# Two outlook layers: 32 by 32 turns on VectorE, regrouped channels and one matmul per group average

## The chip, the cores and the metric

The kernel runs on one core of one Trainium2 chip. A core has TensorE (matmuls, which write to PSUM), VectorE, ScalarE and GpSimd for the rest, and SyncE, which here only issues transfers; 16 DMA engines move data between the chip's HBM and SBUF. In profiles they are PE (and PEld for its weight loads), DVE, ACT, POOL and SP. The metric is device microseconds of one launch. Inputs and outputs are float32 in HBM.

## The reference, cut to what matters

The input x is 8 images of 56 by 56 positions with 384 channels. Two layers follow each other, and each adds its result to x. Both begin with a group norm over 32 groups of 12 channels, whose mean and variance run over all positions of an image.

```python
def gn(v):                                   # per image and group of 12 channels
    return (g - mean(g)) / sqrt(var(g) + 1e-5)

# layer 0: 12 heads of 32 channels, 3x3 window, fold
v = gn(x) @ Wv.T
a = softmax((gn(x) @ Wa.T).reshape(b, n, 12, 9, 9) * 32 ** -0.5)
out = einsum('bnhpq,bnqhd->bnphd', a, windows(v))
y = sum of out[p] shifted to place p of the window     # canvas.at[...].add
x = x + y @ Wo.T

# layer 1: 6 heads of 64 channels, 3x3 window
a = softmax((gn(x) @ W_attn + b_attn).reshape(b, n, 6, 9))
v = gn(x) @ W_v + b_v
x = x + einsum('bpKhd,bphK->bphd', windows(v), a) @ W_proj + b_proj
```

## The kernel before, in words

Images are taken in pairs: four pairs of 2 x 56 = 112 rows (R), each of 56 columns (W). Matmuls contract over channels, so x is needed with channels on the 128 partitions (three chunks, NCH), while HBM holds it with channels innermost. TensorE turns it: a load puts 112 rows of four columns (a block, XB) on 112 partitions, and `stats_chunk` (line 443) turns one chunk of it with four transposes against the identity into a PSUM tile, which ScalarE copies to SBUF; VectorE's `bn_stats` takes the sums for the norm from the copy. Per block there are three such chunks, per pair 14 blocks. Chunk i holds channels 128 i to 128 i + 127. The turned blocks are kept in HBM (`xTs`, `keep_block`) and are loaded again twice: for the norm (`load`, `normed`) and as the residual (`load_res`).

Since a group of 12 channels can cross a chunk's border, `norm_params` (line 275) averages over groups with seven small matmuls against three matrices `gmat`, once for the mean and once for the variance; it runs once for each pair and layer.

Layer 0 is one loop of 224 + 3 steps, a step for a column (line 918). `attend` does a tile of 128 tokens: three matmul sets for the logits, each followed by VectorE's maximum and subtraction, then ScalarE's exponential, then a set for v. Between the sets other work is put in, in an order written out by hand (`between`, line 938): after the first the turning of the next pair's block (`turned`: one chunk a step from the fourth column of a pair on), the previous column's normalisation (VectorE) and products (GpSimd), and a job; after the second the `fold` matmuls (pw) of an earlier column and the `bn_stats` of the turned chunk; after the third another job. The PSUM banks of the sets are three in turn. Softmax weights and values go to tables in HBM (`ztab0`, `vtab0`) and come back as patches: bands of weights z and values vp, by SyncE. `plan` (line 791) gives the jobs of seven columns their due steps: contractions pc of z and vp (ScalarE copies them to yT), then six projections po (two halves of the columns, three chunks each; `project_out`, line 833), whose result VectorE adds to the residual and writes to HBM (`x1s`). All po of layer 0 have one PSUM buffer, tag "o".

Layer 1 is a loop over 32 groups of seven columns, seven steps each (line 1218), with two jobs a step. `load` brings a group's x1t, `normed` scales it on ScalarE, `attend` does logits and v in one set, `fetch` (line 1143) loads z and vp for the group before the last one and puts its jobs in the queue: contractions two tiles at a time, with the turning of an earlier group's columns between them, then the projections. VectorE adds bias and residual in place in x1t. `turn` (line 1190) turns one column of it back with three transposes into PSUM, ScalarE copies to `ot`, and GpSimd issues the store of a half group, 112 rows of four or three columns with all 384 channels. Layer 1's first contractions are due three steps after their fetch.

Instructions that a helper records carry the helper's line: L118 are matmuls, L121 transposes on TensorE, L133 what VectorE, ScalarE, GpSimd and SyncE are given in a fixed order.

Of the kernel before, what the change touches and what calls it, by code (L numbers as in the profile page):

```python
# [15 lines left out]
def two_outlook_layers(  # L16
# [35 lines left out]
    P = 128  # L52
# [45 lines left out]

    xf = x.rearrange("b y x c -> (b y) x c")
# [12 lines left out]
    xTs = [dram.tile([P, NCH, W * R], F32, name=f"xT_{pair}") for pair in range(NPAIR)]  # L112
# [39 lines left out]
    near = [range(max(0, i - 1), min(NCH, i + 2)) for i in range(NCH)]  # L152
    gmat = [const.tile([P, len(near[i]), P], F32, name=f"gmat_{i}") for i in range(NCH)]
    with tc.tile_pool(name="ps_setup", bufs=2, space=PS) as ps_setup:
        gsel = yT_flat[:G, :C]
        gpsimd.memset(gsel, 1.0)
        gpsimd.affine_select(
            out=gsel, in_=gsel, compare_op=ALU.is_ge, fill=0.0,
            base=0, pattern=[[1, C]], channel_multiplier=-GC,
        )  # L160
        gpsimd.affine_select(
            out=gsel, in_=gsel, compare_op=ALU.is_ge, fill=0.0,
            base=GC - 1, pattern=[[-1, C]], channel_multiplier=GC,
        )
        for i in range(NCH):
            pg = ps_setup.tile([P, C], F32, tag="pg", name=f"pg_{i}")
            matmul(pg, gsel[:, i * P : (i + 1) * P], gsel, start=True, stop=True)
            lo, hi = near[i][0] * P, (near[i][-1] + 1) * P
            nc.vector.tensor_scalar_mul(gmat[i].rearrange("p j c -> p (j c)"), pg[:, lo:hi], 1.0 / GC)
# [93 lines left out]
    def weight(pool, src, n, name, queue=nc.sync):  # L263
        t = pool.tile([P, NCH, n], F32, name=name)
        queue.dma_start(t, src.rearrange("(i p) n -> p i n", p=P))
        return t

    def norm_params(st, name, params, key):

        mv = stat.tile([P, NCH, IMG, 2], F32, tag="mv", name=f"mv_{name}")  # L270

        def over_groups(src, what):
            pg = ps.tile([P, NCH, IMG], F32, tag="t", name=f"p{what}_{name}")
            for j in range(NCH):
                for i in near[j]:
                    matmul(
                        pg[:, j, :], gmat[i][:, j - near[i][0], :], src[:, i, :],
                        start=(i == near[j][0]), stop=(i == near[j][-1]),
                    )
            g = stat.tile([P, NCH, IMG], F32, tag=what, name=f"{what}_{name}")  # L280
            vector.tensor_copy(g, pg)
            return g

        for i in range(NCH):
            for b in range(IMG):
                vector.bn_aggr(mv[:, i, b, :], st[:, i, b, :, :])
        yield
        mean = over_groups(mv[:, :, :, 0], "gmean")

        part = stat.tile([P, NCH, IMG], F32, tag="part", name=f"part_{name}")  # L290
        vector.tensor_sub(part, mv[:, :, :, 0], mean)
        vector.tensor_mul(part, part, part)
        vector.tensor_add(part, part, mv[:, :, :, 1])
        yield
        var = over_groups(part, "gvar")
        std = stat.tile([P, NCH, IMG], F32, tag="std", name=f"std_{name}")
        scalar.activation(std, var, AF.Sqrt, bias=eps_t)
        scale = const.tile([P, NCH, IMG], F32, name=f"scale_{name}")
        vector.reciprocal(scale, std)
        bias = const.tile([P, NCH, IMG], F32, name=f"bias_{name}")  # L300
# [81 lines left out]
    zs = [patch.tile([P, NPY0, PY0 * ROW0], F32, name=f"z_{n}", bufs=1) for n in range(2)]  # L382
# [11 lines left out]
    scalar.dma_start(bo_t, bo1.rearrange("(i p) -> p i", p=P))  # L394
# [25 lines left out]
    def layer0(late, pools):  # L420
# [8 lines left out]
        def block_tile(tag, pair, blk):  # L429
            return io.tile([P, NCH, XB, R], F32, tag=tag, name=f"{tag}_{pair}_{blk}")  # L430

        def stats_load(pair, blk, queue, xr):
            queue.dma_start(xr, xf[pair * R : (pair + 1) * R, blk * XB : (blk + 1) * XB, :])
            xrs[pair, blk] = xr

        def xr_tile(pair, blk):
            return io.tile([P, XB, C], F32, tag="xr", name=f"xr_{pair}_{blk}")[:R]
# [5 lines left out]
        def stats_chunk(pair, blk, i):  # L443

            if blk == 0 and i == 0:
                stats[pair] = stat.tile([P, NCH, IMG, NBLK, 6], F32, tag="st0", name=f"st0_{pair}")
            if i == 0 and pair:
                xts[pair, blk] = block_tile("xt", pair, blk)
            xr, xt = xrs[pair, blk], xts[pair, blk]
            if pair == 0:  # L450
                pt = bank(P, 0, XB * R).rearrange("p (m r) -> p m r", m=XB)
            else:
                pt = ps.tile([P, XB, R], F32, tag="t", name=f"pt_{pair}_{blk}_{i}")
            for j in range(XB):
                transpose(pt[:, j, :], xr[:, j, i * P : (i + 1) * P], ident[:R, :R])
            scalar.copy(xt[:, i], pt)
            yield
            for b in range(IMG):
                vector.bn_stats(stats[pair][:, i, b, blk, :], xt[:, i, :, b * H : (b + 1) * H])
# [6 lines left out]
        def keep_block(pair, blk):  # L466
# [3 lines left out]
                    xTs[pair][:, :, blk * XB * R : (blk + 1) * XB * R],  # L470
                    xts.pop((pair, blk)).rearrange("p i m r -> p i (m r)"),
# [42 lines left out]
        for blk in range(NBLK):  # L514
# [5 lines left out]
            if blk == 1:  # L520
                wv_t = weight(fixed, wv0, C, "wv0_t", sync)
# [783 lines left out]
```

## Time and profile before

| | |
|---|---|
| median of 3 runs | 3312.41 us (3310.95 to 3320.32) |
| the profiled execution | 3315.84 us |
| its span, first to last instruction | 3314.0 us |
| TensorE, mean granted clock | 0.978 of full speed |
| TensorE transposes (L121) | 504 of xr for pairs 1 to 3, 168 of pair 0, 672 of results |
| DMA packets | 554,908, 850.99 MB, mean 257 GB/s; 162,174 of them under 512 B |

A profile lists for each engine what it was busy with and what it waited for. Rows of groups and of the timeline name the line, the engine, the operation, out<-in by the program's tile names, the shape and the count. In the timeline the first two numbers are start and length in us; rows that follow each other may overlap, because TensorE's instructions are pipelined, so what a set costs is the distance from its start to the next start. A bracket at the end is idle time before the row and what ended it. A float32 matmul leaves two records, a transpose one. The DMA share is the mean busy share of 16 engines; packets are contiguous runs.

### The profile page before, as it was taken

The page shows a single profiled execution, that of the slowest core. Times are in us where ns is not written, and L with a number is a line of the kernel's source. Part 1 is how long each engine was busy: PE and PEld are TensorE (multiplying, and loading weights), DVE is VectorE, ACT ScalarE, POOL GpSimd, SP SyncE. Part 2 cuts the span into 40 slices and gives each one's busy share as a digit, 9 for nine tenths or more (in the row PEclk, how much of TensorE's full clock was granted, in tenths as well). Part 3 has the DMA queues.
Part 4 walks back from the last instruction along what each step waited for, and adds up shares of the span by engine and source line. Part 5 has one row for each costly group of instructions (what it writes and reads, how often), then busy time and mean ns, then how long its engine had stood idle before and what let it go on. Part 6 is the DMA issues. An engine that isn't in the chain of part 4 may idle for free. (4 is left out here: it accounts for less than half of the span.)

```text
span 3314.0 us, 75237 instructions
## 1 busy us (share of the span) xinstructions
PE 3183.7 (96%) x28510; PEld 2186.6 (66%) x28510; DVE 1870.4 (56%) x4786; ACT 1366.3 (41%) x3749; POOL 1565.1 (47%) x2375
## 2 busy tenths in 40 slices
PE   7899999999999999999999999899999999999998
PEld 5567767776777667677666667556666666666665
DVE  5667776767777776777666677443333333333332
ACT  4444444444444444444343444234343443434432
POOL 2655555545555554455554555454343443434431
PEclk8899999999999999999999999899999999999999
DMA  9699988979897898899787888877778777787775
GB/s 294 201 308 295 303 274 270 292 258 304 300 315 235 279 308 266 290 294 300 229 257 259 288 253 294 285 240 212 220 215 233 212 216 226 220 222 214 223 215 155
DMA packets 554908, 850.99 MB, mean 257 GB/s; under 512 B 162174, under 2 KB 429954, under 8 KB 550450
## 3 DMA queue, kind: packets, MB, share of 16 engines
q1 hardware_dynamic: 448674, 672.76, 65.0%
q0 software_dynamic: 72016, 155.44, 14.7%
q10 hardware_dynamic: 33856, 17.98, 2.1%
q8 instruction: 225, 3.69, 0.5%
q14 instruction: 137, 1.12, 0.1%
HBM read 514.86 MB, written 322.17 MB: 253 GB/s over the span
## 5 line engine op out<-in xcount | busy, mean ns | idle before, releaser
L118 PE MATMUL bank<-wa_t,xn 128*128 128x288 f32 x3528 | 979.0, 415 | 3.5 <-ACT xn L133 2.1
L133 POOL TENSOR_TENSOR at<-at,den 128x972 f32<-128x972 f32 x196 | 440.5, 2247 | 859.3 <-DVE den L133 522.4
L118 PE MATMUL po<-yT,wo_t 128*128 128x448 f32 (+1 forms) x2304 | 821.0, 496 | 14.5 <-DVE x1t L133 12.0
L118 PEld LDWEIGHTS bank<-wa_t,xn 128*128 128x128 f32 x3528 | 652.9, 192 | 218.3 <-issue 22.2
L118 PEld LDWEIGHTS po<-yT,wo_t 128*128 128x128 f32 x2304 | 426.8, 191 | 296.0 <-issue 186.2
L133 ACT ACTIVATE at<-at 128x972 f32<-128x972 f32 (+1 forms) x228 | 215.8, 946 | 867.9 <-DVE at L133 860.5
L1075 POOL DMA_DIRECT2D at<-lgt x392 | 205.4, 527 | 616.3 <-DVE lgt L133 589.5
L118 PE MATMUL bank<-wc_t,xn 128*128 128x438 f32 x1176 | 477.8, 542 | 0.0
L133 DVE TENSOR_REDUCE mx<-bank 128x36 f32<-128x324 f32 x588 | 285.3, 485 | 340.6 <-PE bank L118 338.5
L118 PE MATMUL bank<-wv_t,xn 128*128 128x384 f32 x1176 | 417.3, 491 | 0.0
L118 PE MATMUL pc<-z,vp 121*32 121x49 f32 (+1 forms) x17664 | 374.7, 218 | 16.5 <-issue 10.3
L118 PEld LDWEIGHTS pc<-z,vp 121*32 121x32 f32 (+1 forms) x17664 | 337.8, 120 | 76.4 <-issue 51.0
L133 DVE TENSOR_TENSOR at<-bank,mx 128x324 f32<-128x324 f32 x588 | 291.4, 496 | 107.6 <-POOL pre L133 44.7
L118 PEld LDWEIGHTS bank<-wc_t,xn 128*128 128x128 f32 x1176 | 212.9, 190 | 169.4 <-issue 160.4
L118 PEld LDWEIGHTS bank<-wv_t,xn 128*128 128x128 f32 x1176 | 223.6, 192 | 134.8 <-issue 12.0
L133 DVE TENSOR_TENSOR lgt<-bank,ba_t 128x54 f32<-128x54 f32 x196 | 42.2, 215 | 455.8 <-PE bank L118 451.2
L133 POOL DMA_DIRECT2D vtab<-v x476 | 290.4, 614 | 14.4 <-issue 8.1
L133 ACT COPY yT<-pc 128x294 f32<-128x294 f32 (+2 forms) x512 | 195.7, 407 | 187.3 <-PE pc L118 186.4
L133 POOL TENSOR_TENSOR pre<-at,at 112x108 f32<-112x108 f32 (+1 forms) x440 | 224.4, 527 | 68.7 <-DMA at<-at 48.8
L133 DVE SCALAR_TENSOR_TENSOR x1t<-po,bo_t,x1t 128x448 f32<-128x448 f32 (+1 forms) x156 | 97.6, 626 | 249.5 <-PE po L118 249.5
L133 ACT COPY ot<-pt 112x384 f32<-112x384 f32 x128 | 61.2, 478 | 411.3 <-PE pt L121 411.0
L331 POOL DMA_DIRECT2D vtab<-v x392 | 211.4, 543 | 11.6 <-DMA vtab<-v 6.4
(118 smaller groups left out, 3279.0 us busy)
## 6 DMA issues: line engine op xcount, KB each, us to landing
z<-ztab SPq DMA_DIRECT2D x64, 2352.0 KB
vp<-vtab SPq DMA_DIRECT2D x64, 1536.0 KB
vp<-vtab SPq DMA_DIRECT2D x64, 945.0 KB
xres<-xT SPq DMA_DIRECT2D x32, 1176.0 KB
ztab<-wts SPq DMA_DIRECT2D x336, 110.2 KB
vtab<-v POOLq DMA_DIRECT2D x108, 336.0 KB, 6.2
xin<-xT SPq DMA_DIRECT2D x52, 672.0 KB
xr<-in_x SPq DMA_DIRECT2D x50, 672.0 KB
```

Of the source, the lines that this page charges most:

```text
L118: tc.keep_in_program_order(nc.tensor.matmul(*args, **kwargs))
L133: return lambda *args, **kwargs: tc.keep_in_program_order(op(*args, **kwargs))
L331: queue.dma_start(bass.AP(table.tensor, table.offset + first, [*([line * step, count] for step, count in rows_of or ((1, rows),)), *([[(R ...
L1075: nc.gpsimd.dma_start(at_of(g_of)[row : row + n, m_of].rearrange("r k h -> r (k h)"), lg[lo : lo + n])
```

## The change

Channels are regrouped and most turning is moved to another engine. Chunk i now holds the channels 3p + i, with p the partition, so that the 12 channels of a group lie on four partitions in each of the three chunks. `norm_params` then needs statistics per partition only (its `bn_aggr` runs over the three chunks), one matrix `gmat`, and one matmul for an average. Scale and bias depend on the partition alone, so `normed` covers all chunks in one instruction. Weights whose rows are channels are loaded accordingly; the columns of the two output weights are sorted by three copies each.

For pairs 1 to 3 the transposes of x are VectorE's, which works on 32 by 32 pieces within a quarter of the partitions. A load of a block becomes four, one for each quarter: a quarter takes 96 channels, and each of its 28 used lanes holds four rows, so HBM is read in runs of 96 channels. One VectorE instruction turns a chunk, in place of four transposes and a copy. Blocks in `xTs` are ordered by column, then chunk; the SBUF block has 128 places a row where 112 are stored. Results of layer 1 are turned in the same way after each projection, into an `ot` with four rows a lane, and stored by four SyncE transfers a half in place of one of GpSimd's. With `turn` gone, the contractions become one tile a job. The po tiles take the tags "o" and "t" in turn in both layers, and `attend` of layer 1 uses three banks.

```diff
+    Q = 32
+    NQ = P // Q
+    QC = NCH * Q
+    NR = 4
+    LANES = R // NR
+    def by_quadrant(ap, r0, col, n, b):
+        first = r0 * W * C + col * C + b * QC
+        return bass.AP(ap.tensor, ap.offset + first, [[W * C, R], [C, n], [1, QC]])
...
         def over_groups(src, what):
-            pg = ps.tile([P, NCH, IMG], F32, tag="t", name=f"p{what}_{name}")
-            for j in range(NCH):
-                for i in near[j]:
-                    matmul(
-                        pg[:, j, :], gmat[i][:, j - near[i][0], :], src[:, i, :],
-                        start=(i == near[j][0]), stop=(i == near[j][-1]),
-                    )
+            pg = ps.tile([P, IMG], F32, tag="t", name=f"p{what}_{name}")
+            matmul(pg, gmat, src, start=True, stop=True)
...
+            for b in range(NQ):
+                queue.dma_start(
+                    xr[b * Q : b * Q + LANES].rearrange("p s m c -> p (s m c)"),
+                    by_quadrant(x, pair * R, blk * XB, XB, b),
+                )
...
-                pt = ps.tile([P, XB, R], F32, tag="t", name=f"pt_{pair}_{blk}_{i}")
-            for j in range(XB):
-                transpose(pt[:, j, :], xr[:, j, i * P : (i + 1) * P], ident[:R, :R])
-            scalar.copy(xt[:, i], pt)
+                vector.transpose(
+                    xt[:, :, i, :].rearrange("p m (k s) -> p s m k", s=NR), xr[:, :, :, i::NCH]
+                )
...
-                    xTs[pair][:, :, blk * XB * R : (blk + 1) * XB * R],
-                    xts.pop((pair, blk)).rearrange("p i m r -> p i (m r)"),
+                    xTs[pair][:, blk * XB : (blk + 1) * XB].rearrange("p m i r -> p (m i) r"),
+                    xts.pop((pair, blk)).rearrange("p m i r -> p (m i) r")[:, :, :R],
...
-                po = ps.tile([P, 4 * R], F32, tag="o", name=f"po_{nm}_{half}_{j}")
+                po = ps.tile([P, 4 * R], F32, tag="ot"[(half + j) % 2], name=f"po_{nm}_{half}_{j}")
...
-                for t in range(0, (NPY1 + n_tile - 1) // n_tile, NC):
-                    jobs.add(due, lambda t=t, f=contract: [f(t + n) for n in range(NC)])
-                    jobs.add(due, turning.pop(0) if turning else lambda: None)
+                for t in range((NPY1 + n_tile - 1) // n_tile):
+                    jobs.add(due, lambda t=t, f=contract: f(t))
...
-            def turn(m):
-                pt = banks[-1][:R, :C] if m % 2 else ps.tile([R, C], F32, tag="t", name=f"pt1_{g}_{m}")
-                for i in range(NCH):
-                    transpose(pt[:, i * P : (i + 1) * P], x1t[:, i, m, :], ident)
-                scalar.copy(fetch.ot[:, m - lo, :], pt)
-                if m == hi - 1:
-                    nc.gpsimd.dma_start(
-                        of[pair * R : (pair + 1) * R, px * PX + lo : px * PX + hi, :],
-                        fetch.ot[:, : hi - lo],
-                    )
+                ot = fetch.ot[:, : NR * (hi - lo) * QC]
+                vector.transpose(
+                    ot.rearrange("p (s m c) -> p s m c", s=NR, c=QC)[:, :, :, j::NCH],
+                    bass.AP(x1t.tensor, x1t.offset + j * T + lo * R,
+                            [x1t.ap[0], [1, NR], [R, hi - lo], [NR, Q]]),
+                )
+                if j == NCH - 1:
+                    for b in range(NQ):
+                        later.append(
+                            lambda b=b: sync.dma_start(
+                                by_quadrant(out, pair * R, px * PX + lo, hi - lo, b),
+                                ot[b * Q : b * Q + LANES],
+                            )
+                        )
...
+    def sort_columns(t, by, i, engine):
+        engine(
+            t[:, i].rearrange("k (j p) -> k j p", j=NCH), by[:, i].rearrange("k (p j) -> k j p", j=NCH)
+        )
```

## The prediction

> **What bounds the kernel now.** I read the engine shares first, then the same split by stage, then the order of TensorE's work inside one stage, and last the DMA queues, since the change touches all of them. The stages are the first statistics pass (0 to 60 us), layer 0 on pairs 0 to 2 (to 1630), layer 0 on pair 3 (to 2150) and layer 1.
>
> ```profile
> PE 3183.7 (96%) x28510; PEld 2186.6 (66%) x28510; DVE 1870.4 (56%) x4786; ACT 1366.3 (41%) x3749; POOL 1565.1 (47%) x2375
> ```
>
> The same by stage, with the mean clock, the DMA engines' busy share and GB/s at the end of each row:
>
> ```profile
> core 0: us, PE busy (x) PEld busy (x) DVE busy (x) ACT busy (x) POOL busy (x), PEclk, DMA share, GB/s
> 0.00:60.00 60.00, 37.28 (x203) 31.56 (x204) 33.71 (x109) 24.21 (x49) 14.79 (x59) 0.77 0.98 303
> 60.00:1630.00 1570.00, 1509.86 (x14226) 1087.99 (x14225) 1123.68 (x2990) 688.42 (x1837) 818.77 (x1096) 0.98 0.86 281
> 1630.00:2150.00 520.00, 491.83 (x5038) 347.81 (x5036) 344.76 (x896) 204.88 (x562) 273.76 (x371) 0.96 0.82 268
> 2150.00:3314.00 1164.00, 1144.74 (x9046) 719.21 (x9046) 368.21 (x793) 448.77 (x1303) 457.81 (x850) 0.99 0.77 217
> ```
>
> TensorE is busy 96% in pairs 0 to 2 and 98% in layer 1. VectorE has room (72% and 32%). The 16 DMA engines have less than they seem to: 86% of pairs 0 to 2. A busy share isn't yet a bound, so the second question is what a transpose costs TensorE. Records overlap, so I take it from start to start in TensorE's timeline, not from durations: first three lines of layer 0, then layer 1.
>
> ```profile
> 1478.55 1.62 PE L118 MATMUL bank<-wa_t,xn 128*128 128x288 f32 x6
> 1480.01 0.55 PE L121 MATMUL pt<-ident,xr 112*128 112x112 f32 x4
> 1480.39 1.87 PE L118 MATMUL po<-yT,wo_t 128*128 128x336 f32 x6
> ...
> 2638.97 0.49 PE L121 MATMUL pt<-ident,x1t 128*112 128x128 f32 x3
> 2639.39 1.61 PE L118 MATMUL pc<-z,vp 90*64 90x56 f32 x48
> 2640.93 2.47 PE L118 MATMUL bank<-wc_t,xn 128*128 128x438 f32 x6
> 2643.24 0.49 PE L121 MATMUL bank<-ident,x1t 128*112 128x128 f32 x3
> 2643.66 1.26 PE L118 MATMUL pc<-z,vp 90*64 90x56 f32 x36
> ...
> 2653.71 0.54 PE L121 MATMUL pt<-ident,x1t 128*112 128x128 f32 x3
> 2654.76 2.52 PE L118 MATMUL po<-yT,wo_t 128*128 128x448 f32 x6 [0.51 <-ACT yT L133]
> ```
>
> The matmuls follow each other without a gap, and a set of transposes takes 0.38 us in layer 0 (1480.01 to 1480.39) and 0.42 in layer 1 (0.33 where a po follows). The last line matters too: where nothing but transposes stands between the last contraction and the projection that reads its yT, TensorE waits for ScalarE's copy. The queues:
>
> ```profile
> q1 hardware_dynamic: 448674, 672.76, 65.0%
> q0 software_dynamic: 72016, 155.44, 14.7%
> q10 hardware_dynamic: 33856, 17.98, 2.1%
> ```
>
> A share of 16 engines over 3314 us, divided by the packets, gives the engine time of one packet: q10 32.9 ns at 531 B, q1 76.8 ns at 1499 B, q0 108 ns at 2158 B. The first two give a line of 8.8 ns + 0.0453 ns/B, and it puts q0 at 106.6 ns. So small packets mostly cost their bytes.
>
> [...] No VectorE transpose is in this trace; the nearest rows are TENSOR_TENSOR of 432 elements at 606 ns and of 216 at 384, about 1.03 ns an element and 160 ns fixed[...]. [...]
>
> **The change part by part.**
>
> 1. *Transposes of x, layer 0, pairs 1 to 3* (done while pairs 0 to 2 are computed): 42 blocks x 3 sets leave TensorE: 126 x 0.385 = 48.5 us. A cross-check: pair 3, which has no sets, repeats its pattern after 512 us (1465.12 to 1977.00) where the earlier pairs need 523; 42 sets are worth 16 us, and that stretch holds two thirds of pair 3. The 168 transposes of pair 0, in the first 48 us, stay.
> 2. *Transposes of results, layer 1*: in one group of seven columns (32 groups) seven sets go, 4 x 0.42 less 0.08 that the entry of pc takes back, and 3 x 0.33, so 2.6 us. Against it stands the new order of the jobs. A contraction now does one tile, and they merge into five runs instead of four: +0.14 (a run costs 0.35 per twelve pairs of passes and 0.14 to start: 1.54 for four, 1.19 for three). And the last contraction stands right before projection (0, 0), with no transposes between: copy 0.31 and the hand-over, about 0.5 us. Net 1.9 x 32 = 60 us.
> 3. *Group averages*: 7 matmuls become 1, for mean and for variance, 8 times. At full clock 14 records take 1.48 us (1011.26 to 1012.74), at half clock some 3. Keeping about 0.3 each and the waits for VectorE's bn_aggr, whose input is the same in fewer instructions, leaves about 22 us.
> 4. *Two buffers for po in layer 0* (tags o and t): TensorE's waits for VectorE's x1t, 12.0 us in 16 places, mostly go: -9. What is late next there is the ztab store of the last columns, unchanged.
> 5. *The end*: ScalarE's copies and the four last sets go; three 0.6 us VectorE turns and four SP issues come: -4. The setup of gmat goes too (first transpose at 7.64), but the first pass is bound by loads (DMA 98%): 0.
> 6. *VectorE gains* 126 turns of 512 elements, 96 of 512 and 96 of 384. [...] An estimate throughout. I take 0.7 and 0.57: 88 us in pairs 0 to 2 (1124 + 88 = 1212 of about 1500, 81%) and 122 in layer 1 (42%). Hidden behind TensorE: in projecting steps of about 11 us VectorE idles 2 to 3.5 us. Behind each turn on VectorE stand normalise, then GpSimd's product and the pw matmul a step later: +0.7 us on the 14 places that already wait 34 us for pre. I allow +6.
> 7. *ScalarE* loses 126 copies (66.0 us), 224 copies (107 us) and two thirds of the norm instructions. It is no bound: 0. *GpSimd* loses 64 store issues (34.6 us): 0.
> 8. *DMA.* Loads of x become 4 issues of 448 packets of 384 B for 112 of 6144: per block 1792 x 26.2 / 16 = 2.9 us against 2.0 by the line[...]. Stores to xT become 1536 packets of 448 B, 2.8 against 2.2. Stores of out become 3136 packets of 384 B a group, 5.1 against 3.5[...]. With fewer, longer runs for xin and xres, 187,000 packets more in all. Pairs 0 to 2: 42 x 1.6 = 67 us; share x span goes from 1350 to 1417 of 1503 (1570 less 48.5 and some 18 of parts 3 and 4) = 94%[...]. Layer 1: 896 + 52 = 948 of 1100 = 86%. In 2 us slices full engines read 1.04, so this fits. The cover is lead time: in layer 1 the z bands are issued at 2693.48 and first read at 2708.72, 15 us for 1979 KB that need about 8; x has three steps (27 us). If that cover is gone, each us of lateness is one of TensorE. I allow +6.
> 9. *SP* gets 126 more load issues and 256 stores at about 0.5 us. Out stores wait for the third turn of a half. Behind them stand the next x1t load, needed five steps later, and the next z, six steps later: 0. They no longer compete from GpSimd's queue while z lands.
>
> 10. *Sorting wo's columns*: three copies of 384 elements on VectorE (layer 0) and three on GpSimd (layer 1), below 1 us each, well before the first projection reads them. The GpSimd copies wait for the load of wo1; GpSimd waits for that load today as well (18.2 us before the clearing of wz), and the logits stored behind it are read ten columns later: 0, and a few us at the turn between the layers if not.
>
> Sum: -48.5 - 60 - 22 - 9 - 4 + 12 = -131.5 from a span of 3314.0, so 3182. The profiled run is 3315.84, 1.84 over its span and 3.4 above the median of 3312.41; so the median should be about 3181. Since the two allowances are estimates from above, I say 3178.
>
> **The rivals.** *Likeliest, 0.66:* as summed, TensorE still the bound, 3140 to 3210.
>
> *DMA fills up in pairs 0 to 2, 0.14.* [...] Against: today slices of 0.92 and 0.93 stand beside a TensorE of 98 to 99.7%. Engine work there is 1350 - 184 (today's x and xT transfers, 42 x 4.4) + 8.7 us per ns of a new packet. Against 1503 x 1.04 it binds from 45 ns on; at 50 ns pairs 0 to 2 take 1540 and the kernel about 3215 to 3230. Range to 3290.
>
> *VectorE's order delays TensorE, 0.10.* At 2 us a turn VectorE is at 92%, and three banks no longer cover every step: 3195 to 3260. It is the bound outright from (1503 - 1124)/126 = 3.0 us.
>
> *Slower, 0.08:* packets of 384 B into and out of HBM cost far more than the line says, so that DMA bounds both layers. Work is 1166 + 8.7p in pairs 0 to 2 and 896 - 112 + 6.3p in layer 1; at a capacity of 1.04 both stages together take today's 2734 us when 1950 + 15p = 2843, p = 59.5 ns, and a little above that it decides. Against: q10's packets, most of them 504 B stores, cost 32.9.
>
> *No change, 0.02:* a loss that happens to meet the gain. That the transposes stay is excluded by the code.
>
> **How the numbers follow.** Within 0.3% (3302 to 3322) is what a measurement can't tell from no change. Faster 0.66 + 0.14 + 0.10 = 0.90, same 0.02, slower 0.08. The range 3140 to 3245 holds the first case, over half of the second and most of the third, some 0.8.
>
> **What would show it.** TensorE's only L121 records left are 168 in the first 50 us; pgmean and pgvar have 16 records each; VectorE transposes read 0.6 to 0.8 us; packets about 742,000; the layer 0 pattern of pairs 0 to 2 repeats after some 505 us instead of 523; a group of layer 1 is 1.9 us shorter and its first po waits about 0.5 us for ACT yT in nearly every group. The prediction is wrong if TensorE waits for VectorE's at or for z and vp, if the DMA share of pairs 0 to 2 reads 1.0 or more throughout, or if the turns take over 1.2 us.

## The result, and the profile after

The changed kernel takes 3285.99 us (median; 3282.16 to 3287.08) against 3316.36 for the kernel before on the same chip (3310.95 to 3324.34): a ratio of 0.990, 95% interval 0.988 to 0.993. It is faster by some 30 us, where 3178 had been predicted and a range of 3140 to 3245. The direction was right; three quarters of the gain are missing, and the time lies outside the range. Of the rivals only "DMA fills up" reaches so far (its range went to 3290), and its working, engines full throughout pairs 0 to 2, isn't what the profile shows.

The profiled execution has a span of 3284.7 us. First its page, the busy time of each engine:

```profile
PE 3075.8 (94%) x27136; PEld 2050.6 (62%) x27136; DVE 2180.1 (66%) x5070; ACT 1024.8 (31%) x2736; POOL 1531.7 (47%) x2319
```

TensorE's work did leave: 1374 matmuls and 108 us of busy time less. But the span fell by 29 us only, so TensorE now stands idle for 79 us more. Two of the stages as in the prediction, layer 0 on pairs 0 to 2 and layer 1, in the table of windows (PE, PEld, DVE, ACT, POOL busy; then TensorE's clock, DMA share, GB/s):

```profile
60.00:1630.00 1570.00, 1453.32 (x13445) 1013.39 (x13446) 1234.47 (x3076) 549.82 (x1440) 806.47 (x1080) 0.97 0.90 279
...
2150.00:3314.00 1164.00, 1092.16 (x8459) 654.90 (x8452) 556.65 (x983) 264.70 (x759) 428.84 (x794) 0.98 0.84 221
```

In pairs 0 to 2 TensorE's share fell from 96% to 93%; VectorE's rose from 72% to 79%, the DMA engines' from 0.86 to 0.90. Neither reads like a bound. (A mean share says little of single stretches: in 283 of the 524 slices of 2 us in pairs 1 and 2 the DMA engines read 1.0 or more, and in 256 of 522 before.) To see where the loss is, cut the time at two instructions that both kernels have, the first wa product (layer 0 begins) and the first wc product (layer 1 begins), and set the prediction's sum beside it. Its steps are sorted into these stages, of the sixteen averages two to the start, twelve to layer 0 and two to layer 1, where its own norm stands:

| stage | before | after | change | predicted |
|---|---|---|---|---|
| start, to the first wa product | 59.4 | 63.6 | +4.2 | -3 |
| layer 0, to the first wc product | 2093.0 | 2101.2 | +8.2 | -62 |
| layer 1 and the end | 1161.6 | 1119.9 | -41.7 | -67 |
| whole span | 3314.0 | 3284.7 | -29.3 | -131.5 |

Layer 0 gained nothing at all: it became longer, although 48 us of transposes had left it. That is the main question. "A pair" below is the time from one pair's pgmean of x to the next pair's: 522.4 and 523.4 us before, 523.0 and 526.6 after.

Layer 1 is easy to read. TensorE's timeline in one group:

```profile
2608.51 0.56 PE L128 MATMUL pc<-z,vp 90*64 90x56 f32 x12
2609.47 2.52 PE L128 MATMUL po<-yT,wo_t 128*128 128x448 f32 x6 [0.40 <-ACT yT L143]
```

The transposes are gone, and the first po waits for ScalarE's yT, as predicted: over the run that wait is 17.1 us in 33 places. Eight groups take 265.7 us instead of 277.3, that is 1.45 us a group less and not 1.9. The queue of most transfers, as a last view of the page:

```profile
q1 hardware_dynamic: 647890, 711.32, 73.6%
```

745,406 packets in all, where 742,000 were predicted. By the prediction's line (8.8 ns + 0.0453 ns/B) a packet of q1, now 1098 B on average, should take 58.5 ns; the row gives 59.7. So the price of small packets was right, and so was the engines' work: 0.90 of 1570 us is 1413 us, predicted 1417.

### The profile page after: what moved, and what is told of

Its sections match the earlier page's. It is cut to its first block, busy times and chain, and to the rows that moved or that the text cites. A ratio compares the mean times of both kernels' runs of the same rounds, so it can differ in the third digit from the quotient of the medians.

```text
span 3284.7 us, 71903 instructions
## 1 busy us (share of the span) xinstructions
PE 3075.8 (94%) x27136; PEld 2050.6 (62%) x27136; DVE 2180.1 (66%) x5070; ACT 1024.8 (31%) x2736; POOL 1531.7 (47%) x2319
## 2 busy tenths in 40 slices
DMA packets 745406, 850.80 MB, mean 259 GB/s; under 512 B 406287, under 2 KB 632211, under 8 KB 736739
## 3 DMA queue, kind: packets, MB, share of 16 engines
q14 instruction: 134, 1.09, 0.1%
## 5 line engine op out<-in xcount | busy, mean ns | idle before, releaser
L128 PE MATMUL bank<-wa_t,xn 128*128 128x288 f32 x3528 | 994.5, 420 | 32.7 <-DVE at L143 28.8
L128 PE MATMUL po<-yT,wo_t 128*128 128x448 f32 (+1 forms) x2304 | 822.0, 500 | 17.4 <-ACT yT L143 17.1
L128 PEld LDWEIGHTS po<-yT,wo_t 128*128 128x128 f32 x2304 | 438.3, 192 | 316.3 <-issue 191.6
L128 PEld LDWEIGHTS pc<-z,vp 121*32 121x32 f32 (+1 forms) x17664 | 346.7, 122 | 140.3 <-issue 102.0
L128 PE MATMUL pc<-z,vp 121*32 121x49 f32 (+1 forms) x17664 | 387.0, 221 | 19.3 <-DMA z<-ztab 7.7
L143 DVE TENSOR_TENSOR at<-bank,mx 128x324 f32<-128x324 f32 x588 | 291.2, 495 | 143.7 <-ACT pre L143 59.4
L143 DVE SCALAR_TENSOR_TENSOR wide<-po,bo_t,wide 128x448 f32<-128x448 f32 (+1 forms) x156 | 97.4, 624 | 202.2 <-PE po L128 202.1
L143 ACT ACTIVATE wts<-pre,inside 112x48 f32<-112x48 f32 (+4 forms) x672 | 180.1, 357 | 100.1 <-DMA ztab<-wts 52.7
```

The costliest lines, as they stand in the source:

```text
L128: tc.keep_in_program_order(nc.tensor.matmul(*args, **kwargs))
L143: return lambda *args, **kwargs: tc.keep_in_program_order(op(*args, **kwargs))
```

## What the trace of after says about layer 0

The groups of VectorE instructions, each shape apart (busy us, mean ns):

```profile
L143 DVE STREAM_TRANSPOSE xt<-xr 128x512 f32<-128x512 f32 x126 | 139.6, 1108 | 0.0
...
L143 DVE STREAM_TRANSPOSE ot<-wide 128x512 f32<-128x512 f32 x78 | 86.2, 1105 | 2.7
...
L143 DVE STREAM_TRANSPOSE ot<-wide 128x384 f32<-128x384 f32 x78 | 68.6, 880 | 2.8
```

A turn takes 1.11 us and not 0.7. That alone would still fit a mean of 79%. The mean is the wrong number, though: it is taken over steps of two kinds. In a step with a projection TensorE has some 11 us of work, in a step with contractions only some 8.5 (from 398.05 to 407.46 here, less a wait of 0.95). Here is one of the latter, all engines but with lines left out:

```profile
398.29 0.49 DVE L143 TENSOR_TENSOR at<-bank,mx 128x324 f32<-128x324 f32 x1 [1.09 <-ACT pre L143]
...
398.70 1.10 DVE L143 STREAM_TRANSPOSE xt<-xr 128x512 f32<-128x512 f32 x1
...
404.43 1.72 PE L128 MATMUL bank<-wa_t,xn 128*128 128x288 f32 x6 [0.95 <-DVE at L143]
...
405.86 0.49 DVE L143 TENSOR_TENSOR at<-bank,mx 128x324 f32<-128x324 f32 x1
...
406.39 1.01 ACT L143 ACTIVATE at<-at 128x972 f32<-128x972 f32 x1 [7.29 <-DVE at L143]
...
407.31 0.46 ACT L143 COPY v<-bank 128x384 f32<-128x384 f32 x1
...
407.67 0.46 ACT L143 COPY pre<-at 112x108 f32<-112x108 f32 x2
...
408.04 0.49 DVE L143 TENSOR_TENSOR at<-bank,mx 128x324 f32<-128x324 f32 x1 [1.09 <-ACT pre L143]
```

From 398.29 to 408.04 VectorE works without a pause except for one, always the same, 1.09 us: the first subtract of a step writes a buffer of the ring `at` (four buffers), and the last reader of that buffer is ScalarE's copy `pre`, from which a column's weights are made. In ScalarE's order that copy stands behind the exponential and the copy of v, and the exponential waits for VectorE's third subtract (405.86). So VectorE waits for ScalarE, which had waited for VectorE: a loop of 9.75 us, and TensorE (404.43) waits for it, because its banks are emptied late. This wait in the whole run, before and after (us, times, longest):

```profile
DVE at L133 <- ACT pre L133: 16.1, 45, 1.1
...
DVE at L143 <- ACT pre L143: 59.4, 64, 1.8
```

TensorE's waits, from the pgmean of pair 1 to that of pair 3, two pairs, first after:

```profile
PE pw L128 <- ACT pre L143: 13.9, 4, 3.7
...
PE bank L128 <- DVE at L143: 12.1, 18, 1.0
...
PE pgmean L128 <- DVE mv L143: 11.4, 2, 5.7
...
PE pgvar L128 <- DVE part L143: 9.5, 2, 4.7
...
PE pw L128 <- POOL pre L143: 6.3, 6, 1.6
```

and before:

```profile
PE pw L118 <- POOL pre L133: 12.3, 6, 2.5
...
PE pgmean L118 <- ACT xt L133: 7.7, 2, 3.9
```

With the smaller rows these are 65.5 us after and 29.4 before, 18 us a pair more, about what the transposes took. In the stretch of pair 0, from the first wa product to pair 1's pgmean, they are 48.4 and 28.8, and that stretch grew most, from 429.5 us to 443.1. The new waits are for VectorE, or for ScalarE behind it. None is for z or vp, so the packets don't show here under their own name. The experiments had to say whether VectorE is the whole story.

The waits aren't all of it. In layer 0 TensorE's clock was granted at half for 135 us, and for 99 before. The same work then takes longer, as the stretch of pair 0 shows in two kernels that do the same there, this one and seven_averages (below):

```profile
63.59:506.66 443.07, 396.22 (x3260) 272.25 (x3261) 344.21 (x839) 146.30 (x383) 224.50 (x297) 0.95 0.88 271
...
68.69:498.64 429.95, 386.49 (x3261) 265.81 (x3262) 341.50 (x839) 145.90 (x383) 223.97 (x297) 0.98 0.89 274
```

If TensorE is busy all through such a stretch, half of its length is lost (the clock reads 0.50 there): by that estimate, of the 36 us more at half clock, up to 18 of layer 0's missing 70. The clock belongs to what a wait costs: in the traces of before and after, each of the 37 stretches at half clock between the first 70 and the last 60 us (12 and 25) begins during a TensorE wait of over 1 us or within 4 us of its end. Of the 77 such waits 40 have none, and no run changes the clock alone.

## The experiments

Theories: **VectorE** (its order, lengthened by the turn, with the wait for ScalarE, bounds the contraction steps), **DMA** (the small packets slow pairs 0 to 2), and for the rest of the gain the prediction's own steps 2 to 4. Edits are against the changed kernel; a pair is as above; "layer 0" runs from the first wa to the first wc product.

| kernel | median us | ratio to before (95%) | pairs us | layer 0 us |
|---|---|---|---|---|
| after | 3285.99 | 0.990 (0.988-0.993) | 523.0, 526.6 | 2101.2 |
| pre_early | 3256.51 | 0.982 (0.980-0.984) | 517.7, 519.8 | 2074.7 |
| big_packets | 3268.44 | 0.986 (0.984-0.988) | 521.8, 522.4 | 2085.7 |
| short_turns | 3258.10 | 0.983 (0.980-0.985) | 521.2, 518.3 | 2085.0 |
| early_big | 3227.66 | 0.973 (0.971-0.975) | 509.0, 509.8 | 2049.6 |
| early_big_short | 3205.16 | 0.966 (0.964-0.968) | 502.4, 501.8 | 2022.4 |
| early_big_load | 3227.56 | 0.974 (0.971-0.976) | 508.8, 511.9 | 2047.9 |
| double_turns | 3365.20 | 1.014 (1.012-1.016) | 555.4, 554.4 | 2187.5 |
| late_turn | 3280.19 | 0.989 (0.987-0.990) | 522.8, 523.8 | 2099.9 |
| gpsimd_loads | 3270.51 | 0.985 (0.984-0.987) | 518.1, 523.0 | 2087.3 |
| scalar_loads | 3324.12 | 1.002 (1.001-1.003) | 542.0, 545.0 | 2144.3 |
| seven_averages | 3302.93 | 0.995 (0.994-0.997) | 532.1, 531.9 | 2108.6 |
| one_po | 3298.15 | 0.994 (0.993-0.996) | 529.2, 532.5 | 2118.8 |
| pe_turns | 3255.73 | 0.982 (0.980-0.983) | 518.5, 520.1 | 2073.0 |
| mix | 3388.07 | 1.021 (1.019-1.023) | 516.7, 515.5 | 2062.9 |
| mix2 | 3400.73 | 1.025 (1.024-1.027) | 516.2, 515.6 | 2062.9 |
| mix3 | 3233.09 | 0.974 (0.973-0.976) | 516.1, 515.6 | 2061.1 |
| fetch_first | 3232.03 | 0.974 (0.973-0.976) | 516.3, 515.4 | 2063.9 |

### One suspect at a time

**pre_early** takes the wait for ScalarE away and leaves every instruction in place but one copy.

```diff
             for f, t in ((0, -1), (4, 1)):
+                if t > 0:
+                    yield
 ...
                 elif n == 1:
                     next(folding, None)
                     next(turning, None)
+                    for part in summing:
+                        next(part)
```

> ScalarE's copy of presum's part f=0 is done at between(1) and no longer after the exponential; all else as after the change. VectorE theory (VectorE's order, lengthened by a turn of 1.11 us, with its wait of 1.09 us for ScalarE's copy, bounds the steps that contract in pairs 0 to 2): the wait of `at` for `pre` goes from 59 us to under 15 us, a pair falls from 523 to 508-516 us, and the whole goes from 3286 to 3245-3265 us. DMA theory (the small packets slow pairs 0 to 2): within 5 us of 3286, the same time turns up in waits for z or vp.

**big_packets** loads and stores the same bytes in large pieces.

```diff
-            for b in range(NQ):
-                queue.dma_start(
-                    xr[b * Q : b * Q + LANES].rearrange("p s m c -> p (s m c)"),
-                    by_quadrant(x, pair * R, blk * XB, XB, b),
-                )
+            queue.dma_start(
+                xr[:R].rearrange("p s m c -> p (s m c)"),
+                xf[pair * R : (pair + 1) * R, blk * XB : (blk + 1) * XB, :].rearrange("r m c -> r (m c)"),
+            )
 ... and the store of xT as one run of XB * NCH * R elements a lane
```

> In pairs 1 to 3, x is loaded with one transfer of 6144 B a row and xT stored with 5376 B a lane: the same bytes in some 130 thousand packets less, the columns of x in the wrong order; turns and all other work as after the change. DMA theory: pairs 0 to 2 fall from 523-527 to 505-515 us and the whole from 3286 to 3235-3265 us. VectorE theory: 3286 within 6 us, a pair within 2 us of 523-527, although the DMA share there falls from 0.90 to about 0.7.

**short_turns** shortens the turn to a quarter.

```diff
-                    xt[:, :, i, :].rearrange("p m (k s) -> p s m k", s=NR), xr[:, :, :, i::NCH]
+                    xt[:, :, i, :].rearrange("p m (k s) -> p s m k", s=NR)[:, :1], xr[:, :1, :, i::NCH]
 ... and xt in two fixed buffers
```

> VectorE turns only a quarter of each set of x in layer 0 (128 of 512 elements a lane, about 0.44 us instead of 1.11 us); three quarters of x in pairs 1 to 3 are left out, their place holds what stood there. Packets as after the change. VectorE theory: 0.67 us less in 126 steps, those that contract gain it, so a pair falls from 523 to 505-515 us and the whole from 3286 to 3235-3265 us. DMA theory: within 6 us of 3286.

**double_turns** issues each turn twice (`for _ in range(2):` around the transpose), **late_turn** swaps `next(turning, None)` and `weigh()` in `between(0)`.

> Each of layer 0's 126 turns is issued twice, one after the other, all else as after the change. VectorE theory: 1.11 us more in each of those steps, nearly all of it on the path: a pair goes from 523-527 to 555-570 us, the whole from 3286 to 3370-3420 us. DMA theory: VectorE has room (its mean is 80% there): within 20 us of 3286.

> In each step of layer 0 the turn stands behind the normalisation in VectorE's order and no longer ahead of it; the same instructions in the same number. If the turn costs by delaying the denominator, and with it GpSimd's weights and pw: 8 to 25 us less, 3261-3278 us. If it costs as work in VectorE's loop, wherever it stands: within 6 us of 3286. If mx and x1t, now behind it, are what TensorE waits for: 5 to 30 us more.

Measured against 3286: pre_early -29, big_packets -18, short_turns -28, double_turns +79, late_turn -6. Each theory had the other's kernels at zero, and both are wrong in that: each suspect, lifted alone, gives something, and none brings a pair below 517 us, where 508 to 516 or 505 to 515 were expected. big_packets also stays 3 us short of the gain that was expected of it. VectorE's part is shown from both sides: twice the turns cost 79 us for 140 us of extra work, a little less than expected, and a pair grew by 30 us (its 42 turns bring 46). Where the turn stands in VectorE's order hardly matters (late_turn), so it isn't mainly the delay of the denominator but the length of the loop. What stopped pre_early at 518 us is in its list of waits, here the two rows that changed most (after: 59.4 and 52.7 us):

```profile
ACT wts L143 <- DMA ztab<-wts: 127.4, 42, 11.3
...
DVE at L143 <- ACT pre L143: 3.7, 17, 0.5
```

The loop is open, and now ScalarE waits for the store of earlier weights to leave their buffer before it may write the next. The wait has more than doubled; in short_turns the same row reads 151.6. A second limit stood right behind the first.

### Both together, and all three

**early_big** is pre_early with big_packets, **early_big_short** has the short turns as well. No new edits.

> pre_early and big_packets together (the columns of x in the wrong order, as there). If VectorE's loop and the packets are two limits that stand one behind the other, so that lifting one shows the other: the gains of 30 and 17 us add or better, 3225-3242 us, with the waits for ztab<-wts that pre_early shows (4 to 5 us at a time) mostly gone, pairs at 508-514 us. If they are one and the same loss: 3250-3258 us.

> pre_early, big_packets and short_turns together (three quarters of x in pairs 1 to 3 unturned, columns in the wrong order). VectorE theory: with the turn short too, pairs 0 to 2 reach the 505 us that the prediction had, and the whole 3205-3228 us. If VectorE's turn costs nothing once its wait for ScalarE is gone: the same as early_big within 5 us.

early_big gains 58 us, more than the 29 and 18 of its parts: two limits in line. In its waits the row that had grown is small again:

```profile
ACT wts L143 <- DMA ztab<-wts: 40.3, 12, 10.3
```

With the turns short too, 81 us are back, and a pair takes 502 us; the prediction had 505. Pairs 1 and 2 of the kernel after, and of that one, in the table of windows:

```profile
506.66:1029.68 523.02, 491.31 (x4769) 344.39 (x4768) 416.89 (x1042) 185.90 (x488) 271.22 (x365) 0.98 0.91 283
1029.68:1556.24 526.56, 492.71 (x4769) 345.07 (x4768) 416.89 (x1042) 185.41 (x488) 271.42 (x365) 0.97 0.90 281
...
475.17:977.55 502.38, 484.60 (x4769) 343.55 (x4768) 388.62 (x1042) 184.17 (x488) 270.99 (x366) 0.99 0.89 295
977.55:1479.36 501.81, 482.90 (x4770) 342.53 (x4769) 388.25 (x1042) 184.51 (x488) 271.22 (x366) 0.99 0.89 296
```

Of the 45 us between these two pairs and those after, TensorE's own work is 16, at a lower clock and for the same matmuls; the rest is its waits. Layer 0 is now 70.6 us shorter than in the kernel before (2093.0 to 2022.4); the prediction's steps for it, without the two allowances, make 74. So TensorE's side of layer 0 was costed about right. The three things taken away here are what the change costs there, and the first one isn't even part of the change: ScalarE's copy stood in that place before, in a loop that had room.

### Which packets, and by which queue

**early_big_load** is pre_early with the large loads of x, but with the 448 B stores of xT.

> pre_early with x of pairs 1 to 3 loaded by one transfer of 6144 B a row (columns in the wrong order), while xT is still stored in pieces of 448 B: 71 thousand packets less of the 131 thousand that early_big saves. If the packets count by their number: some 54% of the 29 us from pre_early (3256.5) to early_big (3227.7), that is 3238-3244 us. If the 448 B stores alone hurt: 3252-3258 us. If the 384 B loads alone do: 3226-3232 us.

3227.56 against early_big's 3227.66: the loads are all of it, the stores nothing that these runs can tell. The engine time of the packets removed is q1's share: 73.8% of 16 x 3257.6 us in pre_early less 73.1% of 16 x 3226.4 here, 730 us for 72,240 packets, 10.1 ns each. That is a little over the prediction's 8.8 ns, and over 16 engines 46 us. But loads and issues had gone together. By the rows of SyncE's timeline, its issues take some 730 of the 1038 us of pairs 1 and 2 in pre_early, and some 460 of 1021 here. So SyncE's queue, where the weights' stores stand behind four issues of x, was suspect too. **gpsimd_loads** and **scalar_loads** have pre_early's edit, keep the packets and move their issue (here to GpSimd, in the other to `scalar`):

```diff
-                    stats_load(pair + 1, blk + 1, sync, xr_tile(pair + 1, blk + 1))
+                    stats_load(pair + 1, blk + 1, gpsimd, xr_tile(pair + 1, blk + 1))
```

> The same with GpSimd's queue. If SyncE's queue is the cause: 3226-3245 us. If the packets are: 3250-3260 us; 3265 or more if GpSimd, busy half of the time in layer 0, is late with the weights for it.

> pre_early with the loads of x for pairs 1 to 3, 384 B packets and four issues a block as after the change, issued from ScalarE's queue and no longer from SyncE's. If SyncE's queue is what the loads cost (its issues take 730 us of 1038 in pre_early against 461 of 1021 in early_big_load, and the weights' stores stand behind them): most of early_big_load's 29 us, 3226-3240 us, less up to 10 us if the issues delay ScalarE's exponential. If the small packets themselves slow the DMA engines: 3250-3260 us, the time of pre_early.

gpsimd_loads takes 3270.5, 14 us more than pre_early and not less, though SyncE's issues fell to some 530 of 1041 us. The wait that marks this limit hasn't moved:

```profile
ACT wts L143 <- DMA ztab<-wts: 132.1, 39, 14.7
```

So taking these loads out of SyncE's queue doesn't bring the time back. That doesn't clear the queue. From VectorE's last write of a weights tile to the end of the issue of its second store, the mean of pairs 1 and 2 is 5.2 us in pre_early, 2.4 in early_big_load and 3.5 in gpsimd_loads (2.0 before the change). So the stores do stand longer at SyncE in pre_early, and moving the issues takes back over half of that. What takes its place there, later transfers at a DMA share of 0.93 or GpSimd itself, 43 us a pair busier with the issues, no run separates; the 14 us more aren't settled either. Shown is that the loads in pieces of 384 B cost the 29 us; how they divide between queue and transfers stays open. scalar_loads is no test of this: four issues hold ScalarE for 6.26 us in one case (at 600.88), TensorE waits 68.7 us for yT, and the kernel loses 68 us. So ScalarE had no such room, whatever its 31% say.

### The prediction's smaller steps

```diff
-            matmul(pg, gmat, src, start=True, stop=True)
+            for _ in range(7):
+                matmul(pg, gmat, src, start=True, stop=True)
```

> Each of the 16 group averages issues its matmul seven times over, so 14 matmuls an average run again as before the change, all else as after it. The prediction's step 3 (those matmuls stood on TensorE's path): 16 to 22 us more, 3302-3308 us. Theory from the traces (the average's TensorE waits for VectorE on both sides anyway, 31 us in all after the change, and the matmuls filled that wait): 0 to 8 us more, 3286-3294 us, the waits of pgvar for part falling as the matmuls of pgmean fill them.

+17 us (3302.9): the averages' matmuls were on the path, and my theory from the wait list, that they only filled TensorE's wait for VectorE, has fallen. By stage it is 5.1 in the start, 7.4 in layer 0, 4.0 after it; within layer 0 the two pairs are 9 and 5 us longer and the stretch of pair 0 is 13 us shorter, with less time at half clock, so the sum is firmer than its parts.

```diff
-                po = ps.tile([P, 4 * R], F32, tag="ot"[(half + j) % 2], name=f"po_{nm}_{half}_{j}")
+                po = ps.tile([P, 4 * R], F32, tag="o", name=f"po_{nm}_{half}_{j}")
```

> Layer 0's po has one buffer again, all else as after the change. The prediction's step 4: the 9 us that it gave the second buffer come back, 3293-3297 us. VectorE theory: the wait of po for x1t, 12 us in the kernel before, is longer here because a turn stands ahead of x1t in VectorE's order: 10 to 25 us more, 3296-3311 us.

+12 us: the second buffer is worth its 9 us and a little more; the wait of po for x1t is 18.2 us in 17 places with one buffer.

### A version that beats both

**pe_turns** gives layer 0's turns back to TensorE, with single loads and stores and one buffer for po; layer 1 keeps VectorE's.

```diff
-                vector.transpose(
-                    xt[:, :, i, :].rearrange("p m (k s) -> p s m k", s=NR), xr[:, :, :, i::NCH]
-                )
+                pt = ps.tile([P, XB * R], F32, tag="t", name=f"pt_{pair}_{blk}_{i}")
+            pt = pt.rearrange("p (m r) -> p m r", m=XB)
+            for j in range(XB):
+                transpose(pt[:, j, :], xr[:, j, i::NCH], ident[:R, :R])
+            scalar.copy(xt[:, :, i, :], pt)
 ... with single loads and stores, and one buffer for po in layer 0
```

> Pairs 1 to 3 of x are turned by TensorE and copied by ScalarE again, loaded and stored with one transfer each, and layer 0's po has its one buffer again; layer 1, the averages and the statistics stay as after the change. VectorE theory: layer 0 goes back to the 522-523 us of before the change a pair, that is 0 to 5 us less a pair than now, so 3270-3286 us: TensorE's 48 us come back and VectorE's loss of the same size goes. If the change of layer 0 was a gain in itself: over 3300 us.

3255.7, 30 us better than with VectorE's turns and 14 us below what I expected: layer 0 is 20 us shorter than before the change. Of that the averages are worth 7 to 13 (7.4 in layer 0 of seven_averages; twelve sixteenths of its 17); whether the shorter normalisation gives the rest wasn't tested. As layer 0 stood, moving its transposes was worth less than nothing. **mix** adds three small repairs.

```diff
-                for t in range((NPY1 + n_tile - 1) // n_tile):
-                    jobs.add(due, lambda t=t, f=contract: f(t))
+                for ts in ((0,), (1,), (2, 3)) if b == 0 else ((0,), (1,), (2,), (3,)):
+                    jobs.add(due, lambda ts=ts, f=contract: [f(t) for t in ts])
 ... with pe_turns, pre_early, and no vector.memset of the x buffers
```

> pe_turns (TensorE turns x in layer 0), ScalarE's copy moved as in pre_early, the vector memset of the buffers of x left out (nothing reads those lanes then), and layer 1's contractions in 7 jobs instead of 8 for a group, so that the first po has an attend between it and the last contraction. A group of layer 1 falls from 33.2 to 32.8 us, because the first po no longer waits 0.4 us for ScalarE's yT (11 us over 28 groups); the first wa product comes at 59-61 us instead of 63.6; the copy gives 0 to 8 us with TensorE turning. Together 3230-3248 us; 3250 or more if those waits only move.

3388: 143 us lost in layer 1 (1262 us instead of 1119), with TensorE waiting 100.7 us in 28 places for z. I took it for the second image's contraction, one slot earlier than its load.

> As mix, but the two contractions that share a job are the last two of the second image, not of the first. In mix each group waited 3.67 us for z, because the second image's first contraction came one slot earlier than its transfer; here it keeps its slot and only the last contraction moves ahead of an attend. If that wait was the slot's doing: the waits of pc for z (100 us in mix) go back under 10 us, a group of layer 1 takes 32.7-32.9 us, and with the 17 us that mix showed in the start and layer 0 the whole is 3225-3238 us. If seven jobs as such bring z too late: over 3300 us again.

3401, so that was wrong. Then the waits of SyncE's own queue in a stretch of layer 1 (2377 to 2900 us, some fourteen groups), first mix2:

```profile
SPq L143 <- DVE wide L143: 206.2, 11, 19.8
```

With one job less in a group, the third turn of the first half and its store of out come one slot earlier, and that puts the store ahead of the next group's z and vp in SyncE's order. The store waits for VectorE's turned result, and the loads wait behind it. Two ways out: **mix3** adds `jobs.add(due, lambda: None)` ahead of the first po, so that the stores keep their slots; **fetch_first** leaves mix2's jobs and calls `fetch(...)` ahead of `flush()`.

> mix2 with an empty job ahead of the first po, so that from the second po on each job, and with it each store of out, stands in the slot that it has after the change, while the first po still has an attend ahead of it. If the store of out ahead of the loads of z in SyncE's queue is what cost mix and mix2 their 130 us: SyncE's waits for VectorE's turned result (206 us in mix2, between 2377 and 2900 us) are under 20 us, a group of layer 1 takes 32.6-32.9 us and the whole 3225-3238 us. If the merged contractions are at fault: over 3300 us.

> mix2 with the loads of the next group's z and vp issued ahead of the pending store of out, and nothing else moved. If SyncE's queue is the cause, most of mix2's loss goes: 3230-3290 us (the contractions still come one po earlier after these loads than after the change). If the cause is that missing po alone: 3350 us or more.

Both are as quick as hoped: 3233.1 and 3232.0 us, ratio 0.974 to the kernel before, about 53 us better than the change. The same view of mix3:

```profile
SPq L143 <- DMA ztab<-wz: 139.1, 14, 10.9
...
SPq L143 <- DVE wide L143: 6.4, 1, 6.4
```

The 206 us are 6.4; what remains at the top, the wait for ztab, is as long after the change (155.7 us). In fetch_first SyncE still waits 82.8 us there for turned results, but with the loads already issued. That order is what separates it from mix2, by 169 us. Layer 1 of the two:

```profile
2121.39:3397.80 1276.41, 1134.86 (x8344) 681.44 (x8344) 551.59 (x975) 258.23 (x751) 423.27 (x787) 0.94 0.76 197
...
2122.76:3228.40 1105.64, 1073.32 (x8344) 649.76 (x8344) 551.87 (x975) 260.19 (x751) 423.18 (x787) 0.99 0.86 228
```

Over a third of it, 62 us, is TensorE's busy time: the same 8344 matmuls at a lower clock. Layer 1 takes 1110 us in mix3 and 1106 in fetch_first, against 1120 after the change: the first po's wait, hidden behind an attend, was worth some 10 to 14 us. The start is back at 59.0 us.

## Why the prediction went wrong, step by step

**Step 6 failed, in its conclusion more than in its figure.** It put a turn at 0.7 us, an estimate of mine that no trace showed then (the 160 ns and 1.03 ns an element of the TENSOR_TENSOR rows come to 0.69), took over 1.2 as a sign of failure, and hid the turn behind TensorE because VectorE would be 81% busy in pairs 0 to 2. It takes 1.11 us, and VectorE is 79% busy there. The share was right and of no use: "in projecting steps VectorE idles 2 to 3.5 us" holds for projecting steps, and I never looked at the others. There VectorE's work, with a wait of 1.09 us that only a full loop exposes, exceeds TensorE's. The sign named for this failure came: TensorE waits 29.2 us in 40 places for VectorE's `at`, in layer 0 of the kernel after (1.1 in 3 before). The rival "VectorE's order delays TensorE" described this, but asked for 2 us a turn, because it too was worked out from a mean. The allowance of 6 us stood for the delay of the denominator; late_turn gives some 6 us to that, so the size was right and the main mechanism another. And step 7 left ScalarE at 0, as no bound, though it stands in the loop: moving one copy in its order gave 29 us.

**Step 8 had the prices right and the cover wrong.** Packets, ns per packet and engine work came out within some 2%. But it asked whether the engines would be full and took lead time for cover; the transfer that became late was not one of those it named (z, x) but the small store of the weights, whose buffer ScalarE needs back. The packets cost 18 us with VectorE in the way and 29 without, at a mean share of 0.90 to 0.92, not 1.0; 6 were allowed. Part of that is SyncE's queue, which step 9 had at 0. The rival "DMA fills up" is thus partly true, by another criterion; that its range reached 3290 is luck, since its sum was 3215 to 3230 at 50 ns for a new packet, and one of 384 B takes 25.8 in the kernel after. Since these two losses stand in line, no single rival's mechanism gives the measured time: each was priced as if the other weren't there. And both priced a wait at its own length, without the clock behind it.

**Step 1** (48.5) is right as TensorE's work: its busy time in a pair fell by 16 us, from 508.0 to 492.0. With the suspects removed layer 0 shows it with steps 3 and 4: 70.6 of 74. **Step 3**: 17 of 22. **Step 4**: 12 for 9. **Step 2** gave 1.45 us a group for 1.9, 46 us in place of 60: the first po's wait is as predicted (17.1 us over 32 groups, 0.53 each); from start to start over those eight groups, the transposes freed 2.7 us a group, as costed, and the contractions, cut into more runs, take 0.23 more, where 0.14 was costed. What is missing is in the other matmuls, those of wc, po and pw: the same in number, they take 0.5 us a group longer without the transposes between them. **Step 5** had the end at -4; from 3209.24 before and 3177.93 after to the end it takes 104.8 and 106.8 us, +2, with one wait of 1.97 us for z and 17.1 us at half clock right behind it; and the start, costed at 0, lost 4 us to a wait that step 9 should have listed: SyncE's first load behind VectorE's memset of its buffer (its issue went from 0.81 to 2.56 us, and the first transpose from 7.64 to 14.90). pe_turns, with the memset, has its first wa product at 64.3, mix3, without it, at 59.0. The rest of **steps 7, 9 and 10** shows no loss of its own, but nothing tested it alone. An issue of x costs SyncE 1.23 us on average in the kernel after, though (164 issues), not 0.5.

Of the missing 102 us, layer 0 has 70, layer 1 and the end 25, the start 7. In layer 0 the three suspects account for all of it; in layer 1 the groups for 14 and the end for 6, and the rest wasn't traced.

## What to carry to other kernels

Before work is moved to an engine with room, list that engine's work step by step, for the kind of step where the bounding engine has least to do, and follow its loops through other engines and rings of buffers: a mean of 79% hid steps that were full. When two resources fill up at once, price them in line and not as rivals; lifting one shows the other, and only a kernel with both lifted gives the full amount (58 us here, where each alone gave 29 and 18). In a queue served in order, a store that waits for a result must not stand ahead of a load: that order alone was worth 169 us. And a wait of TensorE costs more than its length where its clock drops behind it: a set of po products took 4.64 us there and 2.36 at full clock.

## What the runs showed of the hardware

VectorE's transpose of 4-byte elements takes 413 ns for 128 elements a lane (short_turns), 880 for 384 and 1106 for 512: 0.18 us fixed and 1.81 ns an element, nearly twice the 1.03 ns of the TENSOR_TENSOR rows. An issue of 448 packets of 384 B occupies SyncE for 0.88 us in the median (pre_early) and 112 packets of 6144 B for 0.48 (early_big_load); GpSimd takes 0.91 for the former (gpsimd_loads). And engine time of packets isn't their whole cost: with 46 us of it over 16 engines, at a mean share of 0.92, the loads in pieces cost 29 us, by their issue and their transfers together.

TensorE's clock reads 1.00 or 0.50 in the traces of before and after, and away from the start and the end (37 stretches) one at 0.50 lasts 3.4 us or two to five times that and begins in or behind a wait of TensorE. In the kernel after, for one, a wait of 1.37 us for yT ends at 2909.20; from 2908.51 to 2915.33 the clock is 0.50, and the set of po products that begins at 2909.20 takes 4.64 us to the next start, where the one at 2310.98, at full clock, takes 2.36.
